# Score stacks of q2 and k2 written straight from PSUM, with weight casts and output blocks shared out anew, in a graph attention kernel

## The chip, the cores and the metric

The kernel runs on one core of one Trainium2 chip. The metric is the device time of one execution in microseconds, as the median over several runs. The engines are named as in the profile: PE (matrix products), DVE, ACT and POOL (vector, scalar and general work), SP (which here only issues DMAs). Each engine takes its instructions strictly in the order in which they were written; they meet at semaphores.

## What is computed

One layer of graph attention over N = 384 nodes, 1024 features, 16 heads of D = 64. The part of the reference that matters:

```python
h = jnp.maximum(_layernorm(x, axis=-1), 0.0)
q = h @ wq.T + bq                      # k and v alike
q2 = (q @ wiq.T + biq).reshape(N, H, D).transpose(1, 0, 2)   # k2 and v2 alike
mask = _build_mask(edge_index, edge_type, edge_type_weights, x.dtype)
scores = jnp.einsum('hnd,hmd->hnm', q2, k2) * scale + mask[None]
attn = jax.nn.softmax(scores, axis=-1)
out = jnp.einsum('hnm,hmd->hnd', attn, v2).transpose(1, 0, 2).reshape(N, OUT_F)
return x + out @ wo.T + bo
```

## The kernel before

**Precision.** A float32 value is kept as a pair: hi, rounded to PE's fast format, and lo, the remainder. A product of two pairs takes three matmuls (hi hi, hi lo, lo hi), written by `mm3` (lines 374 to 376). So each weight chunk of 128 x 1024 is loaded (`load`, line 69), cast to hi (`split_hi`, line 81 on ACT or line 79 on DVE) and subtracted to lo (`split_lo`, line 86, on DVE or POOL). Four such pairs are in flight; chunk w + 2 is cast at the head of chunk w.

**Stages.** After the layer norm come, in this order, v, q, v2 and k: all eight 128-row chunks of each, with the adjacency mask built beside them on POOL and DVE. From about 145 us on come the chunks of q2 and k2 in turn, `iq` and `ik` of pair p = 0 to 7 (a chunk has 128 rows, two heads of 64). A chunk is 24 matmuls, eight of `colmm` at three each.

**The stacks.** For a score, q2 and k2 of a head are laid out over all 128 partitions, so that one matmul sums two products. The q stack of a pair, `qs`, holds for each head hi in one half of the partitions and lo in the other. The k stack `ks` holds hi in both halves, and lo in both halves. `do_S(i)` (line 711) then needs two matmuls per 128 x 384 tile of scores. Before the change a chunk is evacuated by `evac` into `nat`: one ACT instruction writes hi (line 384), one DVE instruction lo (line 385), each over 128 partitions. DMAs (lines 580 to 583 for q, 590 for k) copy the halves from `nat` to the stack, on SP's queue except for pair 0, where ACT's queue takes half of them. `qs` and `ks` have two buffers each, so pair p reuses the buffer of pair p - 2.

**The loop.** A written-out loop of steps i orders everything from the first score on. Tile i is row block t = i % 3 of head h = i // 3. Step i issues, in this order:

- PE: some chunk matmuls, the two score matmuls S(i), more chunk matmuls (`fill`), then PE transposes of two normalised tiles (line 758) and the product with v2 (line 773), every third step;
- DVE: `do_ttr(i - 1)`, which adds the mask, writes the row minimum and so empties the score's bank (line 717); PSUM has two such banks (`"s"`);
- ACT and DVE: the exponential of tile i - 2 (line 721), the reciprocal of tile i - 3 (line 734) and its normalisation, on POOL for t = 1, 2 (line 738); tiles with t = 0 are scaled into two float16 planes (line 744 on ACT, line 748 on DVE) and transposed by a DMA (line 752);
- ACT and DVE: the transposed tiles of step i - 1 leave PSUM as pairs (lines 766, 767, twice each), and the head's output of step i - 1 leaves its bank (`do_ao`, lines 793 on ACT and 794 on DVE);
- at the end of the step the tasks: when a chunk began in this step, `qk_head` evacuates the chunk before it (`qk_done`), orders the cast of chunk w + 2 and loads chunk w + 5. The q chunk of pair p is evacuated at the end of step 6p - 8 for p = 2 to 7, the k chunk at the end of step 6p - 5. The last score that reads the q stack of pair p - 2 is S(6p - 7).

When the q2 and k2 chunks are used up, `fill_o` takes their place in the loop: the output product `out @ wo.T`, in blocks a = 0 to 5 of 128 x 512 (row block, half of the columns), each summed over the eight chunks k of `wo` in two halves of four. `omm` (three matmuls) is one block and one chunk. Three banks `"g"` hold blocks; when a block's first half is complete, `ysum` (line 663, DVE) adds it to the residual and so empties the bank. `flush_y` orders these sums. `wo_prep(k)` casts chunk k of `wo` at the steps `WSTEPS`, `wready` says from which step on it may be used.

Of the kernel before, what the change touches and what calls it, by code (L numbers as in the profile page):

```python
# [26 lines left out]
def gnn_kernel(ctx: ExitStack, tc: tile.TileContext, x, edges, erows, etw, wq, wk, wv, wiq, wik, wiv, wo,  # L27
# [6 lines left out]
    nc = tc.nc  # L34
# [36 lines left out]
    def split_hi(w, dst=None, dve=False):  # L71
        if w >= NCH:
            return
        if dst is None:
            t = wpool.tile([128, 2, D], F32R, tag="whl", name="whl", bufs=4)
            dst = (t[:, 0, :], t[:, 1, :])
        whl[w] = dst
        if dve:
            nc.vector.tensor_copy(dst[0], raw[w])
        else:  # L80
            nc.scalar.activation(dst[0], raw[w], AF.Copy)  # L81
# [301 lines left out]
    def evac(ps, hi, lo, bias):  # L383
        nc.scalar.activation(hi, ps[:, :N], AF.Identity, bias=bias)
        nc.vector.scalar_tensor_tensor(lo, ps[:, :N], bias, hi.bitcast(F32), op0=OP.add, op1=OP.subtract)
# [7 lines left out]
    w = 0  # L393
# [123 lines left out]
        w += 1  # L517

    def v2_early():
        t = work.tile([128, 2, N], F32R, tag="nat", name="tv", bufs=2)  # L520
# [46 lines left out]
    ao = gtile("g1")  # L567
    stacks = {}
    gps = {}

    def qk_done(w):
        n, p = chunks[w]
        q2 = nc.scalar if p == 0 else nc.sync
        nat = work.tile([128, 2, N], F32R, tag="nat", name="nat", bufs=2)
        evac(gps[w], nat[:, 0, :], nat[:, 1, :], bc[:, (3 if n == "iq" else 4) * 8 + p:(3 if n == "iq" else 4) * 8 + p + 1])
        nf = nat.bitcast(F32)
        if n == "iq":
            qs = work.tile([128, 2, N], F32R, tag="qs", name="qs")
            qf = qs.bitcast(F32)
            nc.sync.dma_start(qf[0:64, 0, :], nf[0:64, 0, :])  # L580
            q2.dma_start(qf[64:128, 0, :], nf[0:64, 1, :])
            nc.sync.dma_start(qf[0:64, 1, :], nf[64:128, 1, :])
            q2.dma_start(qf[64:128, 1, :], nf[64:128, 0, :])
            stacks["q", p] = qs
        else:
            ks = work.tile([128, 2, 2, N], F32R, tag="ks", name="ks")
            kf = ks.bitcast(F32)
            for o in range(2):
                for r in range(2):
                    (q2 if r else nc.sync).dma_start(kf[r * 64:(r + 1) * 64, o, :, :], nf[o * 64:(o + 1) * 64, :, :])  # L590
            stacks["k", p] = ks

    tasks = []

# [32 lines left out]
    W0 = 32  # L627
    WO = NCH - 8

    DT = (0,)  # L630
# [74 lines left out]
    def do_S(i):  # L705
        h, t = divmod(i, 3)
        p, o = divmod(h, 2)
        qs, ks = stacks["q", p], stacks["k", p]
        ps = st_ps[i] = bank("s")
        for s in range(2):  # L710
            nc.tensor.matmul(ps[:, :N], qs[:, o, t * 128:(t + 1) * 128], ks[:, o, s, :], start=(s == 0), stop=(s == 1))  # L711

    def do_ttr(i):
        t = i % 3
        e = es[i] = work.tile([128, N], F32, tag="e", name="e", bufs=EB)
        s = sts[i] = work.tile([128, 4], F32, tag="s", name="s", bufs=12)
        nc.vector.tensor_tensor_reduce(e, st_ps.pop(i)[:, :N], ma[:, t, :], -0.125, 3.0e38, OP.add, OP.min, s[:, 0:1])  # L717

    def do_exp(i):
        s = sts[i]  # L720
        nc.scalar.activation(es[i], es[i], AF.Exp, bias=s[:, 0:1], scale=-1.0, accum_out=s[:, 1:2])  # L721

    ptv, plv = [], []

    def pt_setup():
        for _ in range(2):
            f = work.tile([128, 2, NT, N], F32, tag="pt", name="pt").rearrange("p a k n -> p (a k n)").bitcast(F16)
            ptv.extend(f[:, j * 6 * N:(j + 1) * 6 * N].rearrange("p (c n) -> p c n", c=6) for j in range(2))
        f = ptv.pop()
        plv.extend(f[:, 2 * j:2 * j + 2, :] for j in range(3))  # L730

    def do_norm(i):
        s = sts[i]
        nc.vector.reciprocal(s[:, 2:3], s[:, 1:2])  # L734
        if i % 3 in DT:
            nc.vector.tensor_scalar(s[:, 2:3], s[:, 2:3], PSC, None, op0=OP.mult)
        else:
            nc.gpsimd.tensor_tensor(es[i], es[i], s[:, 2:3].to_broadcast([128, N]), OP.mult)  # L738

    planes = {}  # L740

    def do_high(i):
        planes[i] = plv[i // 3 % 3]
        nc.scalar.activation(planes[i][:, 0, :], es[i], AF.Copy, scale=sts[i][:, 2:3])  # L744

    def do_low(i):
        pl = planes[i]
        nc.vector.scalar_tensor_tensor(pl[:, 1, :], es.pop(i), sts[i][:, 2:3], pl[:, 0, :], op0=OP.mult, op1=OP.subtract)
# [71 lines left out]
    t_at, a_at = {}, {}  # L820
    for h in range(16):
        for t in (1, 2):
            t_at.setdefault(3 * h + 7 if h < 15 else 3 * h + 5 + t, []).append(3 * h + t)
        a_at[3 * h + 10 if h < 15 else 3 * h + 9] = h
    for i in range(S + 11):
        now[0] = i
        r = RATE if len(gens) == 2 else RATE_O if i < S else RATE_E
        fill(r / 2)
        if i < S:
            do_S(i)  # L830
        fill(r / 2)
        if 0 <= i - 1 < S:
            do_ttr(i - 1)
        if 0 <= i - 4 < S and (i - 4) % 3 in DT:
            do_low(i - 4)
        if 0 <= i - 2 < S:
            do_exp(i - 2)
        if 0 <= i - 3 < S:
            do_norm(i - 3)
            if (i - 3) % 3 in DT:  # L840
                do_high(i - 3)
# [8 lines left out]
        if 0 <= i - 4 < S and (i - 4) % 3 in DT:  # L850
# [63 lines left out]
```

## Time and profile before

| what | us |
|---|---|
| median of 3 runs (lowest, highest) | 294.54 (294.42, 294.67) |
| the profiled execution, whole | 294.56 |
| its span, first to last instruction | 292.8 |

Busy time of the engines by stretch of the span, in us:

| stretch | length | PE | DVE | ACT | POOL | DMA engines, mean share |
|---|---|---|---|---|---|---|
| v chunks, 15.80 to 49.45 | 33.65 | 33.65 | 26.54 | 18.08 | 20.84 | 0.84 |
| k chunks, 111.25 to 144.68 | 33.43 | 33.43 | 28.84 | 15.15 | 20.15 | 0.48 |
| first q2 and k2 chunks, 144.68 to 160.28 | 15.60 | 15.60 | 11.03 | 6.27 | 3.39 | 0.59 |
| scores and chunks, 160.28 to 240.00 | 79.72 | 79.72 | 60.55 | 63.03 | 37.68 | 0.85 |
| scores, softmax and output blocks, 240.00 to 286.00 | 46.00 | 44.63 | 30.97 | 27.67 | 21.74 | 0.40 |
| last blocks and the result's DMAs, 286.00 to 292.80 | 6.80 | 3.44 | 2.15 | 0.00 | 0.00 | 0.54 |

The busy time of PE counts each matmul from its start to its modelled end, and matmuls overlap, so a full stretch only says that no gap was longer than one matmul's flight. The granted clock of PE was full in every stretch. A line of the timeline below gives the start, the duration, engine and source line, the operation, what it writes and reads, the shape and how many instructions are merged in it; in brackets stands how long the engine sat idle before it, and what released it. A line of a table of waits gives the instruction that waited, the one it waited for, the time in total, how often, and the longest.

### The profile page before, as it was taken

The page shows a single profiled execution, that of the slowest core. Times are in us where ns is not written, and L with a number is a line of the kernel's source. Part 1 is how long each engine was busy: PE and PEld are TensorE (multiplying, and loading weights), DVE is VectorE, ACT ScalarE, POOL GpSimd, SP SyncE. Part 2 cuts the span into 40 slices and gives each one's busy share as a digit, 9 for nine tenths or more (in the row PEclk, how much of TensorE's full clock was granted, in tenths as well). Part 3 has the DMA queues.
Part 4 walks back from the last instruction along what each step waited for, and adds up shares of the span by engine and source line. Part 5 has one row for each costly group of instructions (what it writes and reads, how often), then busy time and mean ns, then how long its engine had stood idle before and what let it go on. Part 6 is the DMA issues. An engine that isn't in the chain of part 4 may idle for free. (4 is left out here: it accounts for less than half of the span.)

```text
span 292.8 us, 4859 instructions
## 1 busy us (share of the span) xinstructions
PE 284.7 (97%) x1610; PEld 267.4 (91%) x1610; DVE 208.2 (71%) x509; ACT 159.7 (55%) x291; POOL 154.8 (53%) x153
## 2 busy tenths in 40 slices
PE   6999999999999999999999999999999999989995
PEld 5999999999988889999999999999999998868874
DVE  3858996667665452999966768878786876788623
ACT  3894543244331222343643778787878788766510
POOL 3765576437775787992004256262627268636210
PEclk9999999999999999999999999999999999999999
DMA  7799857973463342278438879879797969901105
GB/s 268 248 321 404 292 209 254 323 242 112 143 189 122 121 146 72 72 224 296 154 86 227 241 208 211 212 166 227 166 234 147 254 133 234 230 2 27 27 3 215
DMA packets 33305, 54.60 MB, mean 187 GB/s; under 512 B 17408, under 2 KB 20992, under 8 KB 33280
## 3 DMA queue, kind: packets, MB, share of 16 engines
q1 hardware_dynamic: 30896, 51.90, 61.4%
q0 software_dynamic: 2064, 1.80, 2.2%
q10 hardware_dynamic: 320, 0.59, 0.8%
q8 instruction: 13, 0.21, 0.3%
q14 instruction: 12, 0.10, 0.1%
HBM read 38.30 MB, written 3.39 MB: 142 GB/s over the span
## 5 line engine op out<-in xcount | busy, mean ns | idle before, releaser
L374 PE MATMUL g<-g,whl 128*128 128x384 f32 x312 | 105.8, 339 | 0.0
L376 PE MATMUL g<-g,whl 128*128 128x384 f32 x312 | 104.3, 334 | 0.0
L375 PE MATMUL g<-g,whl 128*128 128x384 f32 x312 | 104.2, 334 | 0.0
L231 POOL DMA_INDIRECT tab<-val,idx x51 | 59.7, 1171 | 32.0 <-issue 11.8
L81 ACT ACTIVATE whl<-raw 128x1024 fp32r<-128x1024 f32 x51 | 53.5, 1050 | 29.8 <-PE g L376 21.1
L86 DVE TENSOR_TENSOR whl<-raw,whl 128x1024 fp32r<-128x1024 f32 x41 | 53.8, 1313 | 20.1 <-ACT whl L81 17.0
L374 PEld LDWEIGHTS g<-g,whl 128*128 128x128 f32 x312 | 58.6, 188 | 0.2
L375 PEld LDWEIGHTS g<-g,whl 128*128 128x128 f32 x312 | 58.6, 188 | 0.0
L376 PEld LDWEIGHTS g<-g,whl 128*128 128x128 f32 x312 | 58.6, 188 | 0.1
L390 ACT ACTIVATE g<-f,bc 128x384 fp32r<-128x384 f32 x24 | 14.8, 618 | 53.7 <-DVE f L389 44.8
L738 POOL TENSOR_TENSOR e<-e,s 128x384 f32<-128x384 f32 x32 | 26.4, 829 | 31.2 <-DVE s L734 23.0
L86 POOL TENSOR_TENSOR whl<-raw,whl 128x1024 fp32r<-128x1024 f32 x11 | 26.3, 2395 | 25.9 <-ACT whl L81 25.0
L721 ACT ACTIVATE e<-e,s 128x384 f32<-128x384 f32 x48 | 29.1, 607 | 2.0 <-DVE s L717 1.2
L717 DVE CUSTOM_DVE_ANT_0 e<-s,ma 128x384 f32<-128x384 f32 x48 | 26.4, 552 | 4.3 <-PE s L711 3.7
L389 DVE TENSOR_TENSOR f<-g,rrow 128x384 f32<-128x384 f32 x24 | 13.3, 554 | 18.0 <-PE g L376 18.0
L773 PE MATMUL a<-pt,vhl 128*128 128x384 f16 x96 | 26.1, 326 | 0.0
L758 PE MATMUL t<-ident,e 128*128 128x128 f32 x96 | 24.9, 272 | 0.0
L711 PE MATMUL s<-ks,qs 128*128 128x384 f32 x96 | 24.5, 335 | 0.0
L767 DVE SCALAR_TENSOR_TENSOR pt<-t,pt 128x384 f16<-128x384 f32 x32 | 16.6, 549 | 8.2 <-ACT pt L766 8.2
L799 POOL TENSOR_TENSOR g<-aof,g 128x384 fp32r<-128x384 f32 x8 | 8.3, 1041 | 25.5 <-ACT g L798 25.5
L711 PEld LDWEIGHTS s<-ks,qs 128*128 128x128 f32 x96 | 17.5, 188 | 0.9
L744 ACT ACTIVATE pt<-e,s 128x384 f16<-128x384 f32 x16 | 9.9, 616 | 15.4 <-issue 9.4
(166 smaller groups left out, 447.0 us busy)
## 6 DMA issues: line engine op xcount, KB each, us to landing
ks<-nat SPq DMA_DIRECT2D x30, 192.0 KB
raw<-in_wv_dram SPq DMA_DIRECT2D x8, 512.0 KB
raw<-in_wq_dram SPq DMA_DIRECT2D x8, 512.0 KB
raw<-in_wiv_dram SPq DMA_DIRECT2D x8, 512.0 KB
raw<-in_wk_dram SPq DMA_DIRECT2D x8, 512.0 KB
raw<-in_wiq_dram SPq DMA_DIRECT2D x8, 512.0 KB
raw<-in_wik_dram SPq DMA_DIRECT2D x8, 512.0 KB
raw<-in_wo_dram SPq DMA_DIRECT2D x8, 512.0 KB
```

The costliest lines, as they stand in the source:

```text
L81: nc.scalar.activation(dst[0], raw[w], AF.Copy)
L86: (eng or nc.vector).tensor_tensor(lo, raw[w], hi.bitcast(F32), OP.subtract)
L231: nc.gpsimd.indirect_dma_start(out=tabs[c // RNG], out_offset=bass.IndirectOffsetOnAxis(ap=idx[:, c:c + 1], axis=0), in_=val[:, c:c + 1], ...
L374: nc.tensor.matmul(ps, lhi, rhi, start=first, stop=False)
L375: nc.tensor.matmul(ps, lhi, rlo, start=False, stop=False)
L376: nc.tensor.matmul(ps, llo, rhi, start=False, stop=last)
L711: nc.tensor.matmul(ps[:, :N], qs[:, o, t * 128:(t + 1) * 128], ks[:, o, s, :], start=(s == 0), stop=(s == 1))
L717: nc.vector.tensor_tensor_reduce(e, st_ps.pop(i)[:, :N], ma[:, t, :], -0.125, 3.0e38, OP.add, OP.min, s[:, 0:1])
L721: nc.scalar.activation(es[i], es[i], AF.Exp, bias=s[:, 0:1], scale=-1.0, accum_out=s[:, 1:2])
L738: nc.gpsimd.tensor_tensor(es[i], es[i], s[:, 2:3].to_broadcast([128, N]), OP.mult)
L758: nc.tensor.transpose(ps[:, k * 128:(k + 1) * 128], es[i][:, k * 128:(k + 1) * 128], ident)
L773: nc.tensor.matmul(ps[:, :N], vhl[:, k, h, :, :], ptv[h % 3][:, 3 * s + k, :], start=(k == 0 and s == 0), stop=(k == 2 and s == 1))
```

## The change

- `qk_done` writes the stacks from PSUM by halves of 64 partitions. For q: hi and lo of each head go directly into their halves of `qs`, four instructions (two ACT, two DVE) and no DMA. For k: hi and lo go into the head's own half; hi is copied to the other half by one DMA per head. The other half of lo isn't a copy any more: the two k stacks live through the whole loop, and that half is set to zero once, by four memsets on POOL. The stack's axes change places. The second score matmul then sums hi lo alone, and the product lo lo is left out.
- Of the chunks that `qk_head` orders (q2 and k2 from the third on, and the first two of `wo`), every second one, those with even number w, is cast on DVE instead of ACT, and all remainders are made on POOL; before, POOL made those of odd chunks and DVE the others.
- The output blocks 0, 1, 2 take their chunks 2 and 3 block by block; the second halves go in the order 0, 1, 3, 4, 2. The sums into the residual are ordered at the end of every step instead of just before a bank is asked for. Chunks 2 and 3 of `wo` are cast at steps 36 and 38 (before: 37 and 40).
- The float16 planes get two more buffers, and the row statistics of a head's three tiles share one tile. `LAG` is 0 and `DT` is (0,), so the steps of the normalisation stay where they were.

```diff
 def qk_done(w):
     n, p = chunks[w]
-    q2 = nc.scalar if p == 0 else nc.sync
-    nat = work.tile([128, 2, N], F32R, tag="nat", name="nat", bufs=2)
-    evac(gps[w], nat[:, 0, :], nat[:, 1, :], bc[:, ...])
-    nf = nat.bitcast(F32)
+    ps, bias = gps[w], bc[:, (3 if n == "iq" else 4) * 8 + p:(3 if n == "iq" else 4) * 8 + p + 1]
     if n == "iq":
-        qs = work.tile([128, 2, N], F32R, tag="qs", name="qs")
-        qf = qs.bitcast(F32)
-        nc.sync.dma_start(qf[0:64, 0, :], nf[0:64, 0, :])
-        q2.dma_start(qf[64:128, 0, :], nf[0:64, 1, :])
-        nc.sync.dma_start(qf[0:64, 1, :], nf[64:128, 1, :])
-        q2.dma_start(qf[64:128, 1, :], nf[64:128, 0, :])
-        stacks["q", p] = qs
+        qs = stacks["q", p] = work.tile([128, 2, N], F32R, tag="qs", name="qs")
     else:
-        ks = work.tile([128, 2, 2, N], F32R, tag="ks", name="ks")
-        kf = ks.bitcast(F32)
-        for o in range(2):
-            for r in range(2):
-                (q2 if r else nc.sync).dma_start(kf[r * 64:(r + 1) * 64, o, :, :], nf[o * 64:(o + 1) * 64, :, :])
-        stacks["k", p] = ks
+        ks = stacks["k", p] = ksb[p % 2]
+    for o in range(2):
+        m, l = slice(o * 64, o * 64 + 64), slice(64 - o * 64, 128 - o * 64)
+        hi, lo = (qs[m, o, :], qs[l, o, :]) if n == "iq" else (ks[m, 0, o, :], ks[m, 1, o, :])
+        nc.scalar.activation(hi, ps[m, :N], AF.Identity, bias=bias[m])
+        if n == "ik":
+            kf = ks.bitcast(F32)
+            (nc.scalar if p == 0 and o else nc.sync).dma_start(kf[l, 0, o, :], kf[m, 0, o, :])
+        nc.vector.scalar_tensor_tensor(lo, ps[m, :N], bias[m], hi.bitcast(F32), op0=OP.add, op1=OP.subtract)
...
+ksb = []
+for j in range(2):
+    ksb.append(work.tile([128, 2, 2, N], F32R, tag="ks", name="ks"))
+    for o in range(2):
+        nc.gpsimd.memset(ksb[j].bitcast(F32)[64 - o * 64:128 - o * 64, 1, o, :], 0.0)
...
 def qk_head(w):
-    split_hi(w + 2)
-    split_lo(w + 2, nc.gpsimd if (w + 2) % 2 == PAR else None)
+    split_hi(w + 2, dve=(w + 2) % 2 == PAR)
+    split_lo(w + 2, nc.gpsimd)
...
-WSTEPS = (37, 40, 42, 44, 47, 51)
-PAR, OPOOL, ODVE = 1, (2, 3, 4, 6), (2,)
+WSTEPS = (36, 38, 42, 44, 47, 51)
+PAR, OPOOL, ODVE = 0, (2, 3, 4, 6), (2,)
...
 def fill_o():
-    first = [(0, 0), (0, 1), (1, 0), (1, 1), (2, 0), (2, 1)]
-    first += [(a, k) for k in (2, 3) for a in range(3)] + [(a, k) for a in range(3, 6) for k in range(KH)]
+    first = [(a, k) for c in (0, 2) for a in range(3) for k in (c, c + 1)]
+    first += [(a, k) for a in range(3, 6) for k in range(KH)]
...
         if k == 0:
-            flush_y(1)
             oacc[OT[a]] = bank("g")
...
-    todo = [(a, k) for k in range(KH, 7) for a in range(5)]
+    todo = [(a, k) for k in range(KH, 7) for a in (0, 1, 3, 4, 2)]
...
         if k == KH:
-            flush_y(1)
             oacc[OT[a]] = bank("gggss"[a])
...
 def do_S(i):
-        nc.tensor.matmul(ps[:, :N], qs[:, o, t * 128:(t + 1) * 128], ks[:, o, s, :], start=(s == 0), stop=(s == 1))
+        nc.tensor.matmul(ps[:, :N], qs[:, o, t * 128:(t + 1) * 128], ks[:, s, o, :], start=(s == 0), stop=(s == 1))
...
 for i in range(S + 11):
...
     if i in WSTEPS:
         wo_prep(wp)
         wready[wp] = i + 2
         wp += 1
+    flush_y()
```

More of the change, by code (lines that the diff above doesn't have):

```diff
@@ L381, in colmm @@
             src[:, 0, k, :], src[:, 1, k, :], k == 0, k == KT - 1)
-    def evac(ps, hi, lo, bias):
-        nc.scalar.activation(hi, ps[:, :N], AF.Identity, bias=bias)
-        nc.vector.scalar_tensor_tensor(lo, ps[:, :N], bias, hi.bitcast(F32), op0=OP.add, op1=OP.subtract)
     def evac_row(ps, hi, lo, bias):
@@ L519, in v2_early @@
     def v2_early():
-        t = work.tile([128, 2, N], F32R, tag="nat", name="tv", bufs=2)
+        t = work.tile([128, 2, N], F32R, tag="nat", name="tv", bufs=1)
         tv = t.bitcast(F32).rearrange("p a n -> p (a n)")[:, :512]
@@ L569, in gnn_kernel @@
     gps = {}
+    ksb = []
[3 more added lines that the diff above has]
+            nc.gpsimd.memset(ksb[j].bitcast(F32)[64 - o * 64:128 - o * 64, 1, o, :], 0.0)
     def qk_done(w):
         n, p = chunks[w]
-        q2 = nc.scalar if p == 0 else nc.sync
-        nat = work.tile([128, 2, N], F32R, tag="nat", name="nat", bufs=2)
-        evac(gps[w], nat[:, 0, :], nat[:, 1, :], bc[:, (3 if n == "iq" else 4) * 8 + p:(3 if n == "iq" else 4) * 8 + p + 1])
-        nf = nat.bitcast(F32)
+        ps, bias = gps[w], bc[:, (3 if n == "iq" else 4) * 8 + p:(3 if n == "iq" else 4) * 8 + p + 1]
         if n == "iq":
-            qs = work.tile([128, 2, N], F32R, tag="qs", name="qs")
-            qf = qs.bitcast(F32)
-            nc.sync.dma_start(qf[0:64, 0, :], nf[0:64, 0, :])
-            q2.dma_start(qf[64:128, 0, :], nf[0:64, 1, :])
-            nc.sync.dma_start(qf[0:64, 1, :], nf[64:128, 1, :])
-            q2.dma_start(qf[64:128, 1, :], nf[64:128, 0, :])
-            stacks["q", p] = qs
-        else:
-            ks = work.tile([128, 2, 2, N], F32R, tag="ks", name="ks")
-            kf = ks.bitcast(F32)
-            for o in range(2):
-                for r in range(2):
-                    (q2 if r else nc.sync).dma_start(kf[r * 64:(r + 1) * 64, o, :, :], nf[o * 64:(o + 1) * 64, :, :])
-            stacks["k", p] = ks
+            qs = stacks["q", p] = work.tile([128, 2, N], F32R, tag="qs", name="qs")
+        else:
+            ks = stacks["k", p] = ksb[p % 2]
[7 more added lines that the diff above has]
+            nc.vector.scalar_tensor_tensor(lo, ps[m, :N], bias[m], hi.bitcast(F32), op0=OP.add, op1=OP.subtract)
     tasks = []
@@ L628, in gnn_kernel @@
     WO = NCH - 8
-    DT = (0,)
+    DT, LAG = (0,), 0
     PRE, RATE, RATE_O, RATE_E = 84, 7.9, 8, 8
-    WSTEPS = (37, 40, 42, 44, 47, 51)
-    PAR, OPOOL, ODVE = 1, (2, 3, 4, 6), (2,)
+    WSTEPS = (36, 38, 42, 44, 47, 51)
+    PAR, OPOOL, ODVE = 0, (2, 3, 4, 6), (2,)
     otile = {}
@@ L715, in do_ttr @@
         e = es[i] = work.tile([128, N], F32, tag="e", name="e", bufs=EB)
-        s = sts[i] = work.tile([128, 4], F32, tag="s", name="s", bufs=12)
-        nc.vector.tensor_tensor_reduce(e, st_ps.pop(i)[:, :N], ma[:, t, :], -0.125, 3.0e38, OP.add, OP.min, s[:, 0:1])
+        if t == 0:
+            sts[i // 3] = work.tile([128, 3, 3], F32, tag="s", name="s", bufs=5)
+        s = sts[i // 3][:, 0, t:t + 1]
+        nc.vector.tensor_tensor_reduce(e, st_ps.pop(i)[:, :N], ma[:, t, :], -0.125, 3.0e38, OP.add, OP.min, s)
     def do_exp(i):
-        s = sts[i]
-        nc.scalar.activation(es[i], es[i], AF.Exp, bias=s[:, 0:1], scale=-1.0, accum_out=s[:, 1:2])
+        h, t = divmod(i, 3)
+        s = sts[h]
+        nc.scalar.activation(es[i], es[i], AF.Exp, bias=s[:, 0, t:t + 1], scale=-1.0, accum_out=s[:, 1, t:t + 1])
     ptv, plv = [], []
@@ L730, in pt_setup, with by_dma, factor @@
         plv.extend(f[:, 2 * j:2 * j + 2, :] for j in range(3))
-    def do_norm(i):
[L733 to L736, printed above, removed]
+        f = work.tile([128, 4, N], F16, tag="pl", name="pl", bufs=1)
+        plv.extend(f[:, 2 * j:2 * j + 2, :] for j in range(2))
+    def by_dma(i):
+        return i % 3 in (DT if i < S - 3 else (0,))
+    def factor(i):
+        return sts[i // 3][:, 2, i % 3:i % 3 + 1]
+    def do_norm(i):
+        h, t = divmod(i, 3)
+        s = sts[h]
+        last = max(c for c in range(3) if by_dma(3 * h + c))
+        if by_dma(i) and t < last:
+            return
+        c = slice(0, t + 1) if by_dma(i) else slice(t, t + 1)
+        nc.vector.reciprocal(s[:, 2, c], s[:, 1, c])
+        if by_dma(i):
+            nc.vector.tensor_scalar(s[:, 2, c], s[:, 2, c], PSC, None, op0=OP.mult)
         else:
-            nc.gpsimd.tensor_tensor(es[i], es[i], s[:, 2:3].to_broadcast([128, N]), OP.mult)
+            nc.gpsimd.tensor_tensor(es[i], es[i], factor(i).to_broadcast([128, N]), OP.mult)
     planes = {}
+    npl = itertools.count()
     def do_high(i):
-        planes[i] = plv[i // 3 % 3]
-        nc.scalar.activation(planes[i][:, 0, :], es[i], AF.Copy, scale=sts[i][:, 2:3])
+        planes[i] = plv[next(npl) % len(plv)]
+        nc.scalar.activation(planes[i][:, 0, :], es[i], AF.Copy, scale=factor(i))
     def do_low(i):
         pl = planes[i]
-        nc.vector.scalar_tensor_tensor(pl[:, 1, :], es.pop(i), sts[i][:, 2:3], pl[:, 0, :], op0=OP.mult, op1=OP.subtract)
+        nc.vector.scalar_tensor_tensor(pl[:, 1, :], es.pop(i), factor(i), pl[:, 0, :], op0=OP.mult, op1=OP.subtract)
     def do_turn(i):
@@ L822, in gnn_kernel @@
         for t in (1, 2):
-            t_at.setdefault(3 * h + 7 if h < 15 else 3 * h + 5 + t, []).append(3 * h + t)
+            if not by_dma(3 * h + t):
+                t_at.setdefault(3 * h + 7 if h < 15 else 3 * h + 5 + t, []).append(3 * h + t)
         a_at[3 * h + 10 if h < 15 else 3 * h + 9] = h
@@ L833, in gnn_kernel @@
             do_ttr(i - 1)
-        if 0 <= i - 4 < S and (i - 4) % 3 in DT:
+        if 0 <= i - 4 - LAG < S - 3 and by_dma(i - 4 - LAG):
+            do_low(i - 4 - LAG)
+        if i - 4 == S - 3:
             do_low(i - 4)
@@ L839, in gnn_kernel @@
             do_norm(i - 3)
-            if (i - 3) % 3 in DT:
-                do_high(i - 3)
+        for j in [i - 3 - LAG] if i - 3 - LAG < S - 3 else []:
+            if j >= 0 and by_dma(j):
+                do_high(j)
+        if i - 3 == S - 3:
+            do_high(i - 3)
         turns_and_av(t_at.get(i, []), [a_at[i]] if i in a_at else [])
@@ L849, in gnn_kernel @@
         run_tasks()
-        if 0 <= i - 4 < S and (i - 4) % 3 in DT:
+        if 0 <= i - 4 - LAG < S - 3 and by_dma(i - 4 - LAG):
+            do_turn(i - 4 - LAG)
+        if i - 4 == S - 3:
             do_turn(i - 4)
```

## The prediction

> **What bounds the kernel now.** I first read the page's busy shares.
>
> ```profile
> PE 284.7 (97%) x1610; PEld 267.4 (91%) x1610; DVE 208.2 (71%) x509; ACT 159.7 (55%) x291; POOL 154.8 (53%) x153
> ```
>
> A busy PE isn't yet a full one, so I read the timeline next: in the score stage (160 to 240 us) the 384-column matmuls start 0.17 us apart without a break, at 159.76, 159.93, 160.10. PE's issue is the bound. Time comes back only where PE waits now, and is lost only where a new wait reaches PE. The table of PE's waits has four rows, and one lies in what is changed; in the timeline it is one gap.
>
> ```profile
> PE g L374 <- DVE res L663: 1.4, 1, 1.4
> ```
>
> ```profile
> 258.37 0.51 PE L711 MATMUL s<-ks,qs 128*128 128x384 f32 x2
> ...
> 259.51 0.69 DVE L663 TENSOR_TENSOR res<-g,res 128x512 f32<-128x512 f32 x1
> ...
> 260.25 0.50 PE L374 MATMUL g<-whl,g 128*128 128x512 f32 x1 [1.37 <-DVE res L663]
> ```
>
> After the score at 258.37 the next matmul was due at 258.72 (two steps of 0.17). It started at 260.25, when the sum L663 had emptied its bank: 1.5 us. Third, the waits of SP's queue in the score stage (window 158 to 240 us):
>
> ```profile
> SPq L580 <- PE s L711: 19.3, 6, 3.9
> ```
>
> Six times the first copy into a q stack waits for a score matmul, 19.3 us in all. That costs nothing now, because SP's queue stands still for it and nobody waits for SP. The timeline shows one of the six with the work around it (PE's chunk matmuls left out).
>
> ```profile
> 192.42 0.56 ACT L384 ACTIVATE nat<-g,bc 128x384 fp32r<-128x384 f32 x1
> 192.89 1.05 ACT L81 ACTIVATE whl<-raw 128x1024 fp32r<-128x1024 f32 x1
> 193.02 0.62 DVE L385 SCALAR_TENSOR_TENSOR nat<-g,bc,nat 128x384 fp32r<-128x384 f32 x1 [0.79 <-ACT nat L384]
> 193.55 0.55 DVE L717 CUSTOM_DVE_ANT_0 e<-s,ma 128x384 f32<-128x384 f32 x1
> 193.83 0.60 ACT L721 ACTIVATE e<-e,s 128x384 f32<-128x384 f32 x1
> 194.43 0.85 ACT L766 ACTIVATE pt<-t 128x384 f16<-128x384 f32 x2
> 194.94 1.02 DVE L767 SCALAR_TENSOR_TENSOR pt<-t,pt 128x384 f16<-128x384 f32 x2 [0.76 <-ACT pt L766]
> 195.16 0.51 PE L711 MATMUL s<-ks,qs 128*128 128x384 f32 x2
> 195.31 0.67 ACT L793 ACTIVATE aot<-a,bc,vsc 64x384 f32<-64x384 f32 x1
> 195.74 0.47 SPq L580 DMA_DIRECT2D qs<-nat  x1
> 196.01 0.61 DVE L794 SCALAR_TENSOR_TENSOR aof<-a,vsc,aot 64x384 f32<-64x384 f32 x1
> 196.54 0.54 DVE L717 CUSTOM_DVE_ANT_0 e<-s,ma 128x384 f32<-128x384 f32 x1
> 196.55 0.51 PE L711 MATMUL s<-ks,qs 128*128 128x384 f32 x2
> 198.46 0.51 PE L711 MATMUL s<-ks,qs 128*128 128x384 f32 x2
> ```
>
> The chunk's evacuation is over at 193.64, yet the copy L580 starts at 195.74, just after the score S17 (195.16, ends 195.67). S17 is the last reader of the q stack of two pairs earlier, whose buffer the copy overwrites.
>
> **Part 1, evacuation into the stacks: the wait moves to ACT.** In the changed program's order and semaphores, ACT's first half (hi0) of q waits for the second matmul of S5, S11, S17, S23, S29 and S35: the same six waits, now at the head of ACT's strict queue. The halves are chained too: DVE's lo0 waits for hi0, ACT's hi1 for lo0, lo1 for hi1. Behind them stand, on ACT, cast L81, exponential L721, L766 twice, L793; on DVE, the row minimum L717, a reciprocal, L767 twice, L794, L717 again. Scores have two banks, so S18 waits for the L717 of S16, and S19 for that of S17. Half instructions keep 384 columns: the 64-partition L794 takes 616 ns (DVE), as L385 does on 128, so I use 0.57 us (L384) and 0.62 us a half.
>
> Pair 4 by these rows. hi0 195.74 (as L580, 0.07 after S17) to 196.31; lo0 196.35 to 196.97; hi1 197.02 to 197.59; lo1 from 197.63; L717 0.53 later (193.02 to 193.55), 198.16 to 198.71; S18 198.76, not 196.55: 2.2 us lost, S18 now 3.6 us after S17. Then ACT, with the spacings of the rows: L81 197.49, L721 198.43, L766 199.03, L793 199.91 to 200.58; DVE's L794 200.62, L717 0.53 later, 201.15 to 201.70; S19 201.75, 6.6 us after S17 where it is 3.3 now: 3.3 us lost in all.
>
> Today the two scores behind the six take, from the L711 rows, 1.9 and 3.3 us (S5 168.77, S6 170.68, S7 172.06), 1.4 and 3.3 (S11 181.47), 1.4 and 3.3 (S17), 1.9 and 3.8 (S23 208.34), 1.9 and 3.3 (S29 222.03), 1.9 and 3.3 (S35 235.72). Pair 2 has no L766 behind its evacuation yet (first transposes at 173.45) and loses the first stop alone, 3.6 - 1.9 = 1.7. The others lose 6.6 less the second number: 3.3 + 3.3 + 2.8 + 3.3 + 3.3 = 16.0. Together 17.7 us.
>
> k stacks: their buffers were last read in an earlier step, so no PE wait, but the four links remain. After S19: L736 at 201.85, L744 202.05, L721 202.57, hi0 203.28, lo1 205.17, the cast L79 now on DVE 205.70, L717 of S19 at 206.3 to 206.85. S21 is due at 201.75 + 4.95 = 206.70, starts 206.9 (0.2 lost). The next L717, behind a reciprocal, L767 twice (1.02) and L794, ends 209.1; S22 is due 206.9 + 1.90 = 208.8 (0.3 lost). 0.5 us in pairs 3 to 6: 2.0. Pair 2 lacks that backlog, and pair 7's k falls among 512-column blocks; I take 0 there, at most 0.5 each.
>
> Four POOL memsets lie in an idle of 19.5 us before 153.12: 0, and at most 4 x 0.41 (L139) uncovered. The k copy reads hi at once. Its landing has no row; the last L590 issue of pair 0 ended at 156.69 and S0 ran at 160.28 without a wait, so it lands within 3.6 us, and scores come some 8 us later: 0. SP sheds eight issues of about 0.55 us a pair and its waits, which PE never felt: 0.
>
> **Part 2, weight casts.** For eight chunks hi goes from ACT (L81, 1.05) to DVE (L79, 0.69) and lo from DVE (L86, 1.23) to POOL (L86, 2.39). The DVE and ACT side is in the schedule above. POOL's result is due two chunks (13.7 us) after its order, done in about 6: 0. Behind it POOL's L738 feeds the transposes: in pair 4 L86 runs 198.6 to 201.0, L738 to 201.8, transposes at 202.6. 0.8 us of cover; uncovered, a PE stop of the excess.
>
> DVE and POOL can collide: L748 usually takes 0.62 us, but 1.75 at 267.88, while POOL's L86 ran from 266.82 to 269.22. The Trainium skill, "SBUF — State Buffer", section "Who interferes with whom", says that a DVE instruction with two SBUF inputs and a GpSimd instruction reading SBUF exclude each other for their whole length; the trace agrees (1.13 us more). By this rule the sum would change only where an added L86 meets an L748. In my schedule it meets L767 and L794, which read PSUM and one SBUF operand: 0, with 8 x 1.13 = 9.0 us as upper bound.
>
> **Part 3, output blocks.** The sum that PE waited for is queued at the end of step 42, its bank asked for in step 45: the 1.5 us go. Casts of output chunks 2 and 3 move one and two steps earlier, and are first used in steps 40 and 41, four and three steps on, where remainder and cast need 3.5 us, under two steps: 0. The new block order only makes banks free earlier: 0. More planes and statistics in one tile per head add no instruction to the loop: 0.
>
> **Sum.** 292.8 + 17.7 + 2.0 - 1.5 = 311.0 us of span. The profiled execution took 294.56, 1.8 us more than its span: 312.8 us. The median is 294.54, so nothing is added for it.
>
> **Rivals.**
> - A: the first stop alone, if ACT catches up before L793. 1.7 + 2.2 + 2.2 + 3 x 1.7 = 11.2, less 1.5: 304.2 us. For it: ACT is busy only 64.2 of 82 us in the window 158 to 240. Against: the chain has no idle link.
> - B: POOL compounds it. L86 drifts onto L748 or delays L738 past 0.8 us: up to 9.0 us more, 321.8. For it: POOL's 2.39 us twice per pair. Against: the schedule keeps them apart.
> - C: PE slows after stops. At the start nine 128-column transposes took 2.0 us (1.4 to 3.4), eleven the next 1.4. If each of 11 stops brought 2 us at half pace, 1.0 each, 11: 324. Against: after 1.37 us idle at 260.25 matmuls kept 0.23 us spacing. The Trainium skill, "TensorE: Matmul & The Clock Gate", section "Part 1: The HAM clock gate", lets the clock halve after an idle window of about 3.4 us. By that rule C doesn't occur, since my stops are 2.2 us or less; no run here shows a longer one.
> - D, the other side: ACT's wait stays hidden as SP's did, and only the 1.5 us go: 293.0 us. It decides if S17's end to S18 fits in today's 0.9 us, which needs the four links (2.4 us) to run beside each other or S16's L717 to stand ahead of them. For it: DVE is idle 19.9 of those 82 us. Against: the queue order. That the copy-free stacks don't do what they say would end here as well.
>
> **How the numbers follow.** Forecast 0.66, A 0.14, B 0.12, C 0.03, D 0.05. The forecast's own range is 308 to 317 (the links' hops of 0.05 us doubled, the 2.0 us absent or doubled). A and half of B are taken in: 303 to 321; C, D and the rest of B stay out. Under 0.2% (0.6 us) a measurement here tells no change. D gives faster 0.05; a loss that happens to equal the 1.5 us, 0.01; all else is slower, 0.94.
>
> **What would show it.** Right: PE's waits list S (scores) behind DVE's row minimum about 11 times, near 2.2 and 1.1 us; ACT idles before the q half until PE's score; SP no longer waits for PE; the wait on L663 is gone. A shows one stop per pair, B an L748 of over 1 us or waits of transposes on POOL, C a PE clock below 9. Wrong altogether: PE unbroken from 160 to 240 us.

## The result, and the profile after

| kernel | median, us | lowest, highest | ratio to before, 95% interval |
|---|---|---|---|
| before, in the same comparison | 294.61 | 294.42, 295.71 | |
| changed | 317.83 | 317.51, 317.92 | 1.0778 (1.0751 to 1.0806) |

The change costs 23.2 us, and the span grew by the same: 292.8 to 316.0 us. The forecast was 312.8 us, 5.0 us short: inside the stated range of 303 to 321, but 0.8 us above the forecast's own range of 308 to 317.

From the page of the changed kernel, the busy shares and the groups of the score matmuls (here L704) and of the new halves (L586, L582); before the last bar stands the busy time in all and the mean of one in ns, behind it the idle time ahead of the group and its main releaser:

```profile
PE 291.5 (92%) x1610; PEld 266.8 (84%) x1610; DVE 216.6 (69%) x525; ACT 164.2 (52%) x299; POOL 176.6 (56%) x165
...
L704 PE MATMUL s<-ks,qs 128*128 128x384 f32 x96 | 26.8, 360 | 18.6 <-DVE s L712 16.6
...
L586 DVE SCALAR_TENSOR_TENSOR qs<-g,bc,qs 64x384 fp32r<-64x384 f32 x16 | 9.9, 617 | 23.3 <-ACT qs L582 23.3
...
L582 ACT ACTIVATE qs<-g,bc 64x384 fp32r<-64x384 f32 x16 | 9.2, 577 | 23.4 <-PE s L704 12.9
```

PE, full before, now idles 16.6 us ahead of score matmuls, and what ends that idle time is DVE's row minimum (L712). ACT's halves idle for PE in turn. PE's waits over the whole span of the changed kernel:

```profile
PE s L704 <- DVE s L712: 16.6, 16, 2.1
```

No line of this table names the output blocks' sum any more (1.4 us before). ACT's waits, window 158 to 262 us:

```profile
ACT qs L582 <- PE s L704: 12.9, 6, 2.8
ACT qs L582 <- DVE qs L586: 4.8, 7, 0.7
```

Six waits on a score, as SP had before, now on ACT; the second row is hi1 behind lo0. The timeline of pair 4 in the changed kernel (chunk matmuls, reciprocals and accumulator reads left out) answers to the stretch from 192 to 198 us that the prediction worked out:

```profile
202.16 0.51 PE L704 MATMUL s<-ks,qs 128*128 128x384 f32 x2
202.71 0.58 ACT L582 ACTIVATE qs<-g,bc 64x384 fp32r<-64x384 f32 x1 [2.29 <-PE s L704]
203.31 0.61 DVE L586 SCALAR_TENSOR_TENSOR qs<-g,bc,qs 64x384 fp32r<-64x384 f32 x1 [3.18 <-ACT qs L582]
203.96 0.58 ACT L582 ACTIVATE qs<-g,bc 64x384 fp32r<-64x384 f32 x1 [0.68 <-DVE qs L586]
204.56 1.06 ACT L81 ACTIVATE whl<-raw 128x1024 fp32r<-128x1024 f32 x1
204.57 0.62 DVE L586 SCALAR_TENSOR_TENSOR qs<-g,bc,qs 64x384 fp32r<-64x384 f32 x1 [0.65 <-ACT qs L582]
205.22 0.56 DVE L712 CUSTOM_DVE_ANT_0 e<-s,ma 128x384 f32<-128x384 f32 x1
...
205.84 0.62 PE L704 MATMUL s<-ks,qs 128*128 128x384 f32 x2 [2.13 <-DVE s L712]
206.24 0.87 ACT L776 ACTIVATE pt<-t 128x384 f16<-128x384 f32 x2
...
207.14 0.67 ACT L803 ACTIVATE aot<-a,bc,vsc 64x384 f32<-64x384 f32 x1
...
207.84 0.61 DVE L804 SCALAR_TENSOR_TENSOR aof<-a,vsc,aot 64x384 f32<-64x384 f32 x1
...
208.38 0.54 DVE L712 CUSTOM_DVE_ANT_0 e<-s,ma 128x384 f32<-128x384 f32 x1
...
208.98 0.61 PE L704 MATMUL s<-ks,qs 128*128 128x384 f32 x2 [0.93 <-DVE s L712]
```

S17 ends at 202.67, hi0 starts 0.04 later; hi0, lo0, hi1, lo1 follow without a free gap, then the row minimum that S18 (205.84) waits for, then cast, exponential, L776, L803, L804 and the row minimum for S19 (208.98). S18 comes 3.68 us after S17 (predicted 3.6), S19 6.82 (predicted 6.6).

The same reading for every pair, from the starts of the score rows in both timelines, in us lost against before:

| stretch | predicted | measured |
|---|---|---|
| q, S(6p-7) to S(6p-5), pairs 2 to 7 | 1.7, 3.3, 3.3, 2.8, 3.3, 3.3: 17.7 | 1.89, 3.53, 3.53, 3.01, 3.54, 3.54: 19.0 |
| k, S(6p-5) to S(6p-1), pairs 2 to 6 | 0, then 0.5 each: 2.0 | 0.30, 0.93, 0.92, 0.90, 0.92: 4.0 |
| k of pair 7, S37 to S41 | 0 | 1.32 |
| S0 to S5 (k of pair 1) | 0 | 0.44 |
| output blocks, S41 to S47 | -1.5 | -1.54 |

Together 23.2, which is 316.0 less 292.8 (before S0 and after S47 it is -0.01).

### The profile page after: what moved, and what is told of

It is laid out like the page before. It is cut to its first block, busy times and chain, and to the rows that moved or that the text cites. A ratio compares the mean times of both kernels' runs of the same rounds, so it can differ in the third digit from the quotient of the medians.

```text
span 316.0 us, 4786 instructions
## 1 busy us (share of the span) xinstructions
PE 291.5 (92%) x1610; PEld 266.8 (84%) x1610; DVE 216.6 (69%) x525; ACT 164.2 (52%) x299; POOL 176.6 (56%) x165
## 5 line engine op out<-in xcount | busy, mean ns | idle before, releaser
L86 POOL TENSOR_TENSOR whl<-raw,whl 128x1024 fp32r<-128x1024 f32 x19 | 47.3, 2487 | 54.5 <-ACT whl L81 25.3
L231 POOL DMA_INDIRECT tab<-val,idx x51 | 58.4, 1145 | 33.2 <-issue 11.6
L81 ACT ACTIVATE whl<-raw 128x1024 fp32r<-128x1024 f32 x43 | 45.3, 1052 | 24.7 <-PE g L376 21.1
L86 DVE TENSOR_TENSOR whl<-raw,whl 128x1024 fp32r<-128x1024 f32 x33 | 43.8, 1327 | 16.8 <-ACT whl L81 16.8
L704 PE MATMUL s<-ks,qs 128*128 128x384 f32 x96 | 26.8, 360 | 18.6 <-DVE s L712 16.6
L704 PEld LDWEIGHTS s<-ks,qs 128*128 128x128 f32 x96 | 16.1, 188 | 26.4 <-DVE s L712 23.4
L747 POOL TENSOR_TENSOR e<-e,s 128x384 f32<-128x384 f32 x32 | 26.6, 837 | 11.7 <-DVE s L743 11.7
L712 DVE CUSTOM_DVE_ANT_0 e<-s,ma 128x384 f32<-128x384 f32 x48 | 26.5, 553 | 1.7 <-PE s L704 1.0
L586 DVE SCALAR_TENSOR_TENSOR qs<-g,bc,qs 64x384 fp32r<-64x384 f32 x16 | 9.9, 617 | 23.3 <-ACT qs L582 23.3
L582 ACT ACTIVATE qs<-g,bc 64x384 fp32r<-64x384 f32 x16 | 9.2, 577 | 23.4 <-PE s L704 12.9
L777 DVE SCALAR_TENSOR_TENSOR pt<-t,pt 128x384 f16<-128x384 f32 x32 | 16.5, 550 | 6.4 <-ACT pt L776 6.3
```

Of the source, the lines that this page charges most:

```text
L231: nc.gpsimd.indirect_dma_start(out=tabs[c // RNG], out_offset=bass.IndirectOffsetOnAxis(ap=idx[:, c:c + 1], axis=0), in_=val[:, c:c + 1], ...
L747: nc.gpsimd.tensor_tensor(es[i], es[i], factor(i).to_broadcast([128, N]), OP.mult)
```

## The experiments

L704 and its like are the score matmuls of each kernel, L712 and its like the row minimum. Kernels are compared by their medians, all beside runs of the kernel before, whose median stayed at 294.59 to 294.74.

**A third q2 buffer.** It takes the reuse wait away and leaves the halves.

```diff
-            qs = stacks["q", p] = work.tile([128, 2, N], F32R, tag="qs", name="qs")
+            qs = stacks["q", p] = work.tile([128, 2, N], F32R, tag="qs", name="qs", bufs=3)
...
-        f = work.tile([128, 4, N], F16, tag="pl", name="pl", bufs=1)
-        plv.extend(f[:, 2 * j:2 * j + 2, :] for j in range(2))
```

> The changed kernel with a third buffer for the q stack (room made by dropping the two added float16 planes, so three as before the change). Theory 'buffer wait' (ACT's first half of q stands behind the score S(6p-7) and holds up everything after it): the evacuation starts about 2 to 3 us earlier, its last remainder ends near the time when one evacuation over 128 partitions ended before, and the scores find their banks empty; 293 to 295 us, PE's waits on the row minimum almost gone. Rival 'links' (the chain of four half instructions is too long by itself, also in the k chunks): the stops behind k's evacuation (about 0.9 us per pair) and the second stop of q stay; 300 us or more. Rival 'load' (more work on POOL, and collisions of POOL and DVE): 305 us or more.

Measured: 304.82 us, ratio 1.0347 (1.0320 to 1.0375). The theory's 293 to 295 us is missed; the rival 'links' (300 or more) came true. The stop at S(6p-6) is gone in all six pairs (0.00 against before). What stays is the stop at S(6p-5), 0.62, 1.13, 1.14, 1.64 and 1.12 us in pairs 3 to 7, and the whole k part (0.91 to 0.93). PE's waits:

```profile
PE s L704 <- DVE s L712: 6.4, 11, 1.5
```

So the buffer's wait is worth 317.83 - 304.82 = 13.0 us, and there is a second cost that it doesn't explain.

**q's evacuation one step later.** Two buffers, but the four halves of q are given out at the end of step 6p - 7, so that S(6p-7) is done by then.

```diff
-            pendq.pop(0)()
+            if now[0] >= 0 and chunks[w - 1][0] == "iq":
+                late.append((now[0], pendq.pop(0)))
+            else:
+                pendq.pop(0)()
...
+        if late and late[0][0] < i:
+            late.pop(0)[1]()
```

> The changed kernel with two q buffers, but q's evacuation of pairs 2 to 7 ordered one step later, at the end of step 6p-7, behind the row minimum that the score S(6p-6) needs. Theory 'buffer wait': the wait on the last reader is nearly over when ACT comes to it, and the next score's bank no longer stands behind it: S(6p-7) to S(6p-6) falls from 3.7 us back to 1.4 or 1.9; 294 to 299 us. Rival 'links': the four links stand in front of the next row minimum all the same, and one stop of about 2 us per pair moves to S(6p-5): 304 to 308 us. Rival 'load': no change, 315 us or more.

Measured: 306.87 us, ratio 1.0422 (1.0393 to 1.0451). Again 'links' came true and the theory (294 to 299) did not. As with the third buffer the stop at S(6p-6) is gone (at most 0.02 us) and 0.77 to 1.67 us stay at S(6p-5) in pairs 3 to 7, with k's 0.9 behind them. Two ways of removing the wait, which share no other edit, lie 2.1 us apart, most of it in pair 2 (1.5 us lost here in its q and k stretches, 0.2 with the third buffer), and leave the same kind of rest: it is the wait, not the buffer count or the planes dropped for it.

**Both hi ahead of both lo.**

```diff
+        los = []
         for o in range(2):
...
-            nc.vector.scalar_tensor_tensor(lo, ps[m, :N], bias[m], hi.bitcast(F32), op0=OP.add, op1=OP.subtract)
+            los.append((m, hi, lo))
+        for m, hi, lo in los:
+            nc.vector.scalar_tensor_tensor(lo, ps[m, :N], bias[m], hi.bitcast(F32), op0=OP.add, op1=OP.subtract)
```

> The changed kernel with both halves of hi ordered before both halves of lo, so that ACT's second half no longer waits for DVE's first; the wait for the score S(6p-7) stays. Theory 'buffer wait': the first stop stays within 0.5 us of its 2.3 and 1.8 us, because it starts at the score's end; ACT goes on 0.6 us sooner, so the second stop falls by about 0.6 us in five pairs and the stops behind k by 0.4: 310 to 315 us. Rival 'links': with ACT and DVE no longer in turn most of the loss goes; below 303 us. Rival 'load': 316 us or more.

Measured: 314.38 us, ratio 1.0676 (1.0646 to 1.0706), 3.4 us below the changed kernel. The first stop keeps its size (S17 to S18 is 2.26 us longer than before; 2.30 in the changed kernel). In the built program lo0 now waits for hi1, as hi1 waited for lo0. All of them read one PSUM bank and write one stack tile, and no run tells which of the two puts them one after the other; that ACT's second L776 and DVE's first L777 write one `pt` tile side by side (until 207.11 and from 206.76 in the changed kernel) speaks for the bank. So DVE's part of the chain isn't shorter; ACT is free earlier by a link. That helps what stands behind on ACT: the second stop falls by about 0.7 us in pairs 5 to 7 (2.34, 2.86, 2.86 against 3.01, 3.54, 3.54 for the two stops together); in pairs 3 and 4 PE ran a while at half pace here (last section), and they lost 3.21 and 3.65 against 3.53 each.

**Third buffer and both hi first together.**

> The changed kernel with a third q2 buffer and both hi instructions given out before both lo, together (the two added float16 planes are dropped for room). With the third buffer alone 11.6 us of loss stayed over the kernel with the output blocks alone (304.8 against 293.2): 5.6 between S(6p-7) and S(6p-5), 3.9 between S(6p-5) and S(6p-1). Theory (buffer wait plus the four links in turn): the links become hi0, hi1 on ACT and lo0, lo1 on DVE, so the second hi is about 0.7 us earlier and each of these two losses falls by more than half: 295 to 299 us, waits of PE on DVE's row minimum under 4 us (6.4 before). Rival 'links are cover' (ACT's and DVE's own work, not the turn-taking, is late): 303 or more, waits unchanged.

Measured: 300.11 us, ratio 1.0186 (1.0152 to 1.0220), between the two cases. The stop at S(6p-5) falls to 0.03, 0.47, 0.47, 1.00 and 0.46 us, but k's 0.86 to 0.90 per pair don't move, against the theory. The timeline of DVE alone around k of pair 4 in this kernel shows why:

```profile
202.98 1.25 DVE L589 SCALAR_TENSOR_TENSOR ks<-g,bc,ks 64x384 fp32r<-64x384 f32 x2 [1.11 <-ACT ks L583]
204.26 0.69 DVE L79 CAST whl<-raw 128x1024 fp32r<-128x1024 f32 x1
204.99 0.56 DVE L715 CUSTOM_DVE_ANT_0 e<-s,ma 128x384 f32<-128x384 f32 x1
```

DVE waits 1.11 us for both hi and works 1.25 us: 2.36. In turn, as DVE's rows around k of pair 4 in the changed kernel have it, it is wait and work twice:

```profile
211.12 0.61 DVE L586 SCALAR_TENSOR_TENSOR ks<-g,bc,ks 64x384 fp32r<-64x384 f32 x1 [0.51 <-ACT ks L582]
212.38 0.62 DVE L586 SCALAR_TENSOR_TENSOR ks<-g,bc,ks 64x384 fp32r<-64x384 f32 x1 [0.65 <-ACT ks L582]
213.03 0.69 DVE L79 CAST whl<-raw 128x1024 fp32r<-128x1024 f32 x1
213.76 0.56 DVE L712 CUSTOM_DVE_ANT_0 e<-s,ma 128x384 f32<-128x384 f32 x1
```

0.51 + 0.61 + 0.65 + 0.62 = 2.39 us, no more than 0.03 apart. For k it makes no difference in which order the links stand; their number does.

**Halves into `nat`.** The kernel before with the second and third parts of the change, its evacuation into `nat` cut into two halves, all DMAs and buffers as before.

```diff
-        evac(gps[w], nat[:, 0, :], nat[:, 1, :], bc[:, ...])
+        for o in range(2):
+            m = slice(o * 64, o * 64 + 64)
+            evac(gps[w][m], nat[m, 0, :], nat[m, 1, :], bias[m])
```

> The kernel before with the second and third parts, and with its evacuation into the buffer of its own cut into two halves of 64 rows (hi0, lo0, hi1, lo1 for q and for k); all DMAs, buffers and stacks as before. Theory (what is left with a third q2 buffer, 304.8 us, is the doubled evacuation on ACT and DVE and nothing of stacks, copies or DMAs): 302 to 306 us, with stops of PE on the row minimum of 1.0 to 1.6 us in each pair from the third on, none at S(6p-6). Rival 'the direct stacks and their DMAs matter' (the halves alone are covered): 293 to 297.

Measured: 304.87 us, ratio 1.0358 (1.0329 to 1.0388). It is the third-buffer kernel again (304.82), stretch by stretch: 0.65, 1.13, 1.13, 1.63, 1.11 for q, 0.90 to 0.92 for k, and the same row of waits.

```profile
PE s L712 <- DVE s L718: 6.4, 11, 1.4
```

So the second cost, 304.87 - 293.16 (the kernel with the output blocks alone, below) = 11.7 us, comes without any change to a stack, a copy or a DMA. The two kernels differ in the cut into halves and in the new casts. The casts cost nothing by themselves and save time where halves are (both below), so the 11.7 us are the halves' with the new casts beside them; no run has them with the old ones and the old stacks. And 13.0 + 11.7 = 24.7 is all of 317.83 - 293.16.

**q alone and k alone.** One stack written from PSUM by halves, the other made through `nat` as before.

```diff
+        if n == "iq":    # k direct alone; the other kernel has "ik" and the four copies of k
+            nat = work.tile([128, 2, N], F32R, tag="nat", name="nat", bufs=2)
+            nc.scalar.activation(nat[:, 0, :], ps[:, :N], AF.Identity, bias=bias)
+            nc.vector.scalar_tensor_tensor(nat[:, 1, :], ps[:, :N], bias, nat.bitcast(F32)[:, 0, :], op0=OP.add, op1=OP.subtract)
...
+            nc.sync.dma_start(qf[0:64, 0, :], nf[0:64, 0, :])
...
+            return
```

> The changed kernel with q2's stack made as before (one 128-row evacuation into a buffer of its own and four DMAs), k2's stack written from PSUM by halves with its one copy per head (the two added float16 planes are dropped for room). Theory (q's buffer wait and q's links make 19 of the 24.6 us, k's links about 4): 296 to 299 us, S(6p-7) to S(6p-5) back to 3.3 us in pairs 3 to 7. Rival 'k is only late behind q': 293 to 295, since k's own four links are hidden. Rival 'any direct evacuation loads ACT and DVE': 303 or more.

> The changed kernel with k2's stack made as before (one 128-row evacuation into a buffer of its own and four DMAs), q2's stack written from PSUM by halves into its two buffers (the two added float16 planes are dropped for room). k's direct evacuation alone cost 3.2 us (296.4 against 293.2). Theory (q's stop 19 us, and k's evacuation by halves eats a cushion that the stop has already used up): the stops S(6p-7) to S(6p-6) and S(6p-5) stay at 3.5 to 3.8 and 6.6 to 7.0 us, the 0.9 us per pair between S(6p-5) and S(6p-1) falls to 0.3 or less: 311 to 314.6 us. Rival 'the k part is late through q' (the 0.9 stay): 316 to 318.

Measured: k alone 296.36 us, ratio 1.0075 (1.0045 to 1.0104); q alone 313.00 us, ratio 1.0640 (1.0608 to 1.0673). Over 293.16 that is 3.2 us for k, 19.8 for q, and 4.8 for k once q is direct (317.83 - 313.00). k alone loses 0.00, 0.00, 0.39, 0.50, 0.93 us in pairs 2 to 6, not 0.9 each: it has a cushion to eat first. In the kernel before, DVE's row around k of pair 4 read:

```profile
199.30 0.62 DVE L385 SCALAR_TENSOR_TENSOR nat<-g,bc,nat 128x384 fp32r<-128x384 f32 x1 [0.52 <-ACT nat L384]
200.24 1.23 DVE L86 TENSOR_TENSOR whl<-raw,whl 128x1024 fp32r<-128x1024 f32 x1 [0.33 <-ACT whl L81]
201.38 0.55 DVE L717 CUSTOM_DVE_ANT_0 e<-s,ma 128x384 f32<-128x384 f32 x1
```

That row minimum ends at 201.93, and the score that needs its bank, S21, comes at 203.41: 1.5 us early. With k direct alone the minimum ends 0.13 us ahead of S21, and 0.06 us ahead of pair 5's S27, which is the bare step from the minimum's end to the score's start (208.92 to 208.98 above); in the changed kernel, where q's stops have used the cushion up, it is 0.06 us at both. q alone has its stops unchanged (19.0 us for both) and only 0.09 to 0.12 us in the k part of pairs 3 to 6. In pair 2 it loses the 0.30 us of the changed kernel, and k alone 0.00: this piece of the k row is q's.

**The casts, taken back and alone.** The second part was undone in the changed kernel, and done alone in the kernel before.

```diff
-        split_hi(w + 2, dve=(w + 2) % 2 == PAR)
-        split_lo(w + 2, nc.gpsimd)
+        split_hi(w + 2)
+        split_lo(w + 2, nc.gpsimd if (w + 2) % 2 == PAR else None)
...
-    PAR, OPOOL, ODVE = 0, (2, 3, 4, 6), (2,)
+    PAR, OPOOL, ODVE = 1, (2, 3, 4, 6), (2,)
```

> The changed kernel with its second part undone: every hi of the weight split on ACT, the remainders on POOL only for every second chunk. Theory (the evacuation makes the loss, the casts nothing): 316.5 to 319.5 us, and the stops before S18, S19 and their like in every pair stay at 3.5 to 3.8 and 6.6 to 7.0 us after S(6p-7). Rival 'casts' (DVE's hi casts and POOL's remainders delay the row minimum or the links): 314 or less, the stops shorter. Third way: ACT, which gets four more hi casts of 0.97 us in the loop at the head of its queue, is later still: 320 or more.

> The kernel before with the second part alone: the hi of every second weight split on DVE, all remainders on POOL. Theory: 294.0 to 295.3 us, no new wait of PE in the loop. Rival 'casts': 296 or more, with waits of PE on the row minimum. If it takes work off ACT that PE was waiting for: 293.5 or less.

Measured: with the old casts the changed kernel takes 323.05 us, ratio 1.0964 (1.0918 to 1.1009), 5.2 us more; alone in the kernel before the new casts take 294.45, ratio 0.9989 (0.9968 to 1.0010). The third way of the first expectation came true, but on DVE. DVE's rows around k of pair 4 with the old casts:

```profile
215.53 0.62 DVE L586 SCALAR_TENSOR_TENSOR ks<-g,bc,ks 64x384 fp32r<-64x384 f32 x1 [0.65 <-ACT ks L582]
216.62 1.22 DVE L86 TENSOR_TENSOR whl<-raw,whl 128x1024 fp32r<-128x1024 f32 x1 [0.46 <-ACT whl L81]
217.87 0.56 DVE L712 CUSTOM_DVE_ANT_0 e<-s,ma 128x384 f32<-128x384 f32 x1
```

From the end of lo1 to the row minimum it is 1.72 us with the old remainder and its wait for ACT's cast (216.15 to 217.87), against 0.76 with DVE's own cast (213.00 to 213.76). The k part grows by the same 0.95 us per pair (0.92 to 1.87). Where the cushion is whole, as in the kernel before, this saves nothing; where halves have eaten it, 0.96 us each.

**Output blocks alone.** The kernel before with the third part.

```diff
-    WSTEPS = (37, 40, 42, 44, 47, 51)
+    WSTEPS = (36, 38, 42, 44, 47, 51)
...
-                flush_y(1)
...
-        todo = [(a, k) for k in range(KH, 7) for a in range(5)]
+        todo = [(a, k) for k in range(KH, 7) for a in (0, 1, 3, 4, 2)]
...
+        flush_y()
```

> The kernel before with part 3 of the change alone (order of the output blocks, sums ordered at the end of each step, output chunks 2 and 3 cast earlier). Theory: the wait of PE on the sum into the residual (1.37 us in the trace, 1.5 us from the time when the matmul was due) goes and nothing takes its place: 292.8 to 293.3 us. Rival: the sum, queued earlier, delays a row minimum and the stop moves to a score: 294 to 295 us.

Measured: 293.16 us, ratio 0.9951 (0.9933 to 0.9968). S41 to S47 is 1.51 us shorter and nothing else moves by more than 0.05. This is the one part that pays, and with it alone the kernel is faster than both.

## Why the prediction was right, and where its sizes were off

- **Part 1, the wait moves to ACT.** Right in place, number and order: six waits, two stops behind each, pair 2 with one. The q term was 17.7 and is 19.0. S18 comes 0.08 us later than worked out, S19 0.22. The missing time is in ACT's spacings, which were taken from the rows of before: there L766 followed the exponential by 0.60 us (193.83 to 194.43), here L776 follows by 0.72 (205.52 to 206.24), and L803, L804 and the row minimum carry that on to S19. The experiments split this term in a way the prediction didn't: without the wait the first stop goes altogether, and the second keeps 0.6 to 1.6 us through the halves.
- **k's four links, 2.0 us.** The mechanism was right, the size half: 4.0. The prediction let S21 and S22 lose 0.2 and 0.3; the rows lost 0.34 from S20 to S21 and 0.35 from S21 to S22. The row minimum for S21 stood 4.78 us after S19 (213.76 less 208.98), not 4.55 (206.3 less 201.75), because the cast L79 and the minimum don't overlap lo1 as the schedule let them. Another 0.11 (S19 to S20) and 0.12 (S22 to S23) are a term that the prediction doesn't have: after a stop the second score matmul starts 0.28 us after the first instead of 0.17 (the pair takes 0.62 us in the row at 205.84, 0.51 at 202.16). Behind S18 and S21 this is lost in the next stop, behind S19 and S22 it counts. The kernel before shows the same behind the wait that part 3 removes, where the prediction read an unchanged spacing of 0.23 us:

```profile
260.25 0.50 PE L374 MATMUL g<-whl,g 128*128 128x512 f32 x1 [1.37 <-DVE res L663]
260.59 0.40 PE L375 MATMUL g<-whl,g 128*128 128x512 f32 x1
260.83 0.40 PE L376 MATMUL g<-whl,g 128*128 128x512 f32 x1
```

  The first step is 0.34 us, the next 0.24. Pair 2, taken at 0, lost 0.30 (q's, as shown above), pair 1, not looked at, 0.44 (0.00 with q alone, so it is k's).
- **Part 2, 0.** Alone it is 0 (0.9989). Inside the changed kernel it gives 5.2 us back; the prediction had this in its k schedule, where L79 stands in place of L86, but called the part free of effect. The bound it gave for this part, up to 9.0 us of loss by collisions (rival B), wasn't drawn on: of the remainders that POOL has to make in addition, only one met L758 (0.87 us at 167.12, and no score behind it came later).
- **Part 3, -1.5.** Exact for the wait: -1.54 in place, and 1.5 us as a kernel of its own (294.69 to 293.16). But of the casts that move earlier, taken as 0, one cost time in pair 7, whose k the prediction took as 0, at most 0.5, without working out its schedule. From DVE's and POOL's rows of the changed kernel:

```profile
263.32 2.38 POOL L86 TENSOR_TENSOR whl<-raw,whl 128x1024 fp32r<-128x1024 f32 x1 [1.07 <-issue]
...
263.57 2.54 DVE L758 SCALAR_TENSOR_TENSOR pt<-e,s,pt 128x384 f16<-128x384 f32 x1
...
266.11 0.59 DVE L586 SCALAR_TENSOR_TENSOR ks<-g,bc,ks 64x384 fp32r<-64x384 f32 x1
```

  L758 takes 0.62 us as a rule, here 2.54: it holds DVE until POOL is done at 265.70, and k's lo0 starts 1.6 us late. S37 to S41 lost 1.32. The remainder is that of `wo` chunk 2, which POOL makes in the kernel before too, but a step later (242.05) and clear of L748 (239.45). With the output blocks alone, so with the old casts of q2 and k2, the two meet as well:

```profile
239.39 2.38 POOL L86 TENSOR_TENSOR whl<-raw,whl 128x1024 fp32r<-128x1024 f32 x1 [0.91 <-issue]
...
239.65 2.54 DVE L746 SCALAR_TENSOR_TENSOR pt<-e,s,pt 128x384 f16<-128x384 f32 x1
```

  There S37 to S41 lost nothing, and with q alone direct, k evacuated whole, they meet too (2.53 us) and the stretch lost 0.10. With the old casts in the changed kernel L758 came 0.06 us ahead of the remainder (0.62 us), and the stretch lost 0.12. It takes both, the collision and the halves. So rival B named the mechanism but looked for it in part 2. The Trainium skill's rule on DVE and GpSimd ("SBUF — State Buffer", section "Who interferes with whom"), cited for it, agrees with these rows.
- **A** had the second stop covered: it wasn't. **D** needed links side by side; the timeline has them one behind the other. **C** was argued away too fast, see the last section; it added nothing measurable here.

In sum the span came out 5.0 us above 311.0: 1.3 for q, 2.0 in the k stretches of pairs 2 to 6, 1.3 for k of pair 7, 0.4 for pair 1. The direction and the place follow from the mechanism; that 317.83 us lies inside the stated range is in part luck, since that range went beyond 317 only to take in half of rival B, while 3.7 of the 5.0 us have nothing to do with a collision.

Left open: hi1 and lo0 read different partitions of one PSUM bank, and the program orders them all the same. The Trainium skill, "PSUM — Partial Sum Buffer", section "PSUM bank collisions raise a hardware error", says that accesses of two engines to different quadrants of a bank may run at the same time. No run here shows that; links side by side were not tried.

## What to carry to other kernels

A wait costs what stands behind it in its queue. On a DMA queue that nobody waits for, 19.3 us of waiting were free; the same six waits at the head of ACT's queue cost 13.0 us of a PE-bound loop, and one more buffer, or issuing one step later, takes them away. Cutting an instruction over 128 partitions into two over 64 doubles its time (0.58 and 0.62 us each, as the whole had), and in this kernel that was free only as long as the row minimum behind it came early: read the cushion (here 1.5 us) before spending it, and expect a second edit to be worth nothing or a microsecond a pair depending on whether it is still there.

## What the runs showed of the hardware

- When PE starts again after a wait, it loses about 0.1 us more: in 22 score pairs of the changed kernel the second matmul follows the first by 0.25 to 0.28 us instead of 0.17; in the kernel before, where no score waits, there is no such pair, but the same 0.1 us stands behind its wait at 260.25 (0.34 us instead of 0.24).
- PE's clock can halve after shorter idling than the prediction allowed. In the kernel with both hi first, these windows (columns: PE, PEld, DVE, ACT, POOL busy and instructions, granted clock, DMA share, GB/s) follow a stop of 2.1 us that began at 185.55:

```profile
186.00:189.00 3.00, 1.36 (x7) 1.36 (x8) 2.64 (x7) 2.93 (x6) 2.08 (x1) 0.95 0.00 0
189.00:192.00 3.00, 3.00 (x11) 3.00 (x10) 2.53 (x9) 2.23 (x6) 1.14 (x3) 0.50 0.01 3
192.00:195.00 3.00, 3.00 (x21) 2.73 (x21) 2.02 (x4) 2.90 (x7) 0.76 (x1) 0.99 0.41 87
```

  For about 3.2 us the 384-column matmuls start 0.32 us apart instead of 0.17; the same happens once more, from 206 to 209 us, and nowhere else in the score stage. That run (mean clock 0.988) took 313.76 us, another of the same kernel at 1.00 took 313.72. In the changed kernel's profiled run stops of the same 2.1 us left the clock at 1.00, in its other runs the mean was 0.988 to 0.995, and the times agree within 0.41 us. The Trainium skill, "TensorE: Matmul & The Clock Gate", section "Part 1: The HAM clock gate", was read in the prediction as needing an idle window of 3.4 us; here PE was idle for 2.1 us, and the half pace began about 1 us after its matmuls had resumed (187.64), so if a window of that length decided it, the window wasn't wholly idle. The same section of the Trainium skill says that the window runs free of the program, which would fit a stop that halves the clock in one run and not in another; the runs don't show the window itself.
